# Third attention on single-pass products of split parts, its seams moved off VectorE, with a pair of unread products in every second unit

## The chip, the cores and the metric

One Trainium2 chip, of which the kernel uses one core. A core has five engines that run beside each other: TensorE (PE, matrix products), VectorE (DVE), ScalarE (ACT), GpSimd (POOL) and SyncE (SP, which issues most of the DMAs). Products are written to PSUM, eight banks of 128 x 512 fp32 each. The metric is the time on the device in microseconds (us), one launch; the lower, the better.

## The reference

The whole program is four layers of an attention and a feed-forward part each, on x of shape (4, 512, 128) in fp32. Three layers and the mixture of experts behind the third attention are untouched. What the change touches is the attention of the last layer, with 16 heads of 8 numbers:

```python
xn = (x - mu) / sqrt(var + EPS) * ln_gamma + ln_beta
q, k, v = split(xn @ W_qkv.T + b_qkv)          # (4, 16, 512, 8) each
scores = q @ k.T / sqrt(8)
probs = softmax(scores)
out = (probs @ v) @ W_out.T + b_out
```

The kernel's x before it comes from a mixture of experts (`f30`), whose two results per token are added first, and its result goes through the router of the next mixture (`f31`). The residual is added in the kernel's own form: x, its normalized rows and the output row are added beforehand, the projected attention last.

## The kernel before

**Units.** `attention` (L601) serves three layers. For the last one (tag `a3_`) it works in 16 units: four batches of 512 rows, and four groups of four heads. The heads of a group lie in four row strips of 32 partitions, so that four products with 32 rows of contraction can run in TensorE at the same time.

**Two passes over the scores.** The softmax needs the largest score of each query before the exponentials. `largest` multiplies q by k with queries on the partitions (`s_a`, 16 products of 32 x 512 a unit), and VectorE reduces each (`low<-s_a`, L721). `lowered` transposes the negated maxima on TensorE (`low_a`, L727) and adds them to q in rows that the heads of this unit leave unused (`ql_a`, L730); k has ones in those rows. `by_key` multiplies the other way round, keys on the partitions (`t_a`, 16 products), so that the maximum is subtracted inside the product, and ScalarE takes the exponentials out of PSUM (`w_a`, L741). `times_values` multiplies them by v and a column of ones (`acc_a`, L837). `summed` copies the sums, `normalized` transposes them (`ot_a`, L856) and divides, `gathered` and `ended` transpose and project a whole batch, and `residual` adds it to x.

**Number format.** `factors` gives fp32 operands, for which TensorE records two instructions a product, unless the unit is in `parts`; then the operands are `fp32r`, one instruction a product. The first attention works that way: q and k are split into a rounded part (hi) and the rest (lo), and the four strips of a head's 32 rows hold hi and lo so that one product makes the sum of the parts' products. The rows take this shape on a round trip through DRAM (`to_units`, `unit_qk`). The third attention passes no `parts` before the change.

**Order.** PE, DVE, ACT and POOL run in the order of the program text in this stage; SP's queue is ordered by a scheduler. A half-round is two products of `largest` for a later unit, two of `by_key` for the current one, interleaved, and the values of an earlier round; eight half-rounds make a unit:

```python
together(step(largest, n + lead), step(by_key, n))
```

with `lead` of ten half-rounds. The first unit has an order of its own (`first_unit`). The loop over units also puts in its pieces of other work: `begin(b)`, a generator that combines the mixture's results, normalizes x, and makes q, k and v of the next batch a piece at a time; `go_on`, the router of `f31` for a finished batch; `normalized`, `gathered`, `ended`; and `beside`, which writes zeros over the DRAM rows of `f31` (two times 2080 KB and once 2048 KB, L285) from SP's queue.

**Per unit.** `start` calls `project`, which masks q on ScalarE (`q_a`, L1019) and k on POOL (`k_a`, L1699) for the unit's group.

Of the kernel before, what the change touches and what calls it, by code (L numbers as in the profile page):

```python
# [9 lines left out]
FP = mybir.dt.float32  # L10
# [32 lines left out]
def kernel(ctx: ExitStack, tc: tile.TileContext, a: dict, out: bass.AP):  # L43
# [202 lines left out]
    class Mixture:  # L246
# [289 lines left out]

        def combine(self, b):

            for j in range(self.k):
                row = 1 + j * T + b * S  # L540
                r = work.tile([P, NT, D], FP, name=f"r{j}{b}_{self.tag}", tag="n", bufs=3)
                nc.sync.dma_start(r, self.res[row : row + S, :].rearrange("(t p) d -> p t d", p=P))
                nc.vector.tensor_tensor(xs[b], xs[b], r, ALU.add)
            yield
# [47 lines left out]

    lows = []

    def rows_of_largest(pool):
        for i in range(2):
            low = pool.tile([P, NT, P], FP, name=f"low{i}", tag=f"low{i}", bufs=1)
            nc.gpsimd.memset(low, 0.0)
            lows.append(low)

    def attention(pool, tag, begin, project, residual, owT, added, after=None, beside=(), fetch=None, parts=None):  # L601

# [17 lines left out]

        def product(ps, q, k, r, i, n0, n1, as_=FP):
            nc.tensor.matmul(  # L622
                ps[:, n0:n1],
                q[r : r + SLOT, i * P : (i + 1) * P].bitcast(as_),
                k[r : r + SLOT, n0:n1].bitcast(as_),
                start=True,
                stop=True,
            )

        def factors(u):  # L630

            if parts is not None and units[u] in parts:
                return *parts[units[u]], FR
            return *st["qk", u], FP
# [75 lines left out]
        def largest(u, i, rs):  # L710
            q, k, as_ = factors(u)
            out = []
            if i == 0 and rs[0] == 0:
                st["low", u] = lows[u % len(lows)]
            for r in rs:
                ps = bank(f"s_{tag}{u}_{i}{r}")
                yield lambda ps=ps, r=r: product(ps, q, k, r * SLOT, i, 0, S, as_)
                out.append((ps, r))
            for ps, r in out:
                c = r * SLOT + (units[u][1] + 1) % NG * HD  # L720
                nc.vector.tensor_reduce(st["low", u][:, i, c : c + 1], ps, AX.X, ALU.max, negate=True)  # L721

        def lowered(u, n0=0, n1=S):
            q, k = st["qk", u]
            ps = bank(f"low_{tag}{u}")
            for i in range(n0 // P, n1 // P):
                nc.tensor.transpose(ps[:, i * P : (i + 1) * P], st["low", u][:, i, :], ident)  # L727
            if n0 == 0:
                st["ql", u] = pool.tile([P, S], FP, name=f"ql_{tag}{u}", tag="ql", bufs=2)
            nc.vector.tensor_tensor(st["ql", u][:, n0:n1], ps[:, n0:n1], q[:, n0:n1], ALU.add)  # L730

        def by_key(u, j, rs):
            q, k = st["qk", u]
            out = []
            for r in rs:
                ps = bank(f"t_{tag}{u}_{j}{r}")
                yield lambda ps=ps, r=r: product(ps, k, st["ql", u], r * SLOT, j, 0, S)
                out.append((ps, r))
            for ps, r in out:
                w = pool.tile([P, S], FP, name=f"w_{tag}{u}_{j}{r}", tag="w", bufs=8)  # L740
                nc.scalar.activation(w, ps, AF.Exp)  # L741
                st["w", u, j, r] = w
# [49 lines left out]
        def first_unit():  # L792
# [19 lines left out]
            together(top[10], other[0, 1])  # L812
            start(2)
            together(top[11], other[0, 0])
            for j in range(2, NT):
# [51 lines left out]
        def gathered(b):  # L867
            oT = pool.tile([P, S], FP, name=f"oT_{tag}{b}", tag="ou", bufs=3)
            copy(oT, transposed(st["o", b].rearrange("p t g c -> p t (g c)"), f"oT_{tag}{b}"))
            st["oT", b] = oT  # L870
# [3 lines left out]
        def ended(b):  # L874
            po = bank(f"proj_{tag}{b}").rearrange("p (t d) -> p t d", d=D)
            for t in range(NT):
                nc.tensor.matmul(po[:, t, :], st["oT", b][:, t * P : (t + 1) * P], owT, start=True, stop=True)
            residual(b, po)
# [3 lines left out]
        def go_on():  # L882
            if rest and next(rest[0], "end") == "end":
                rest.pop(0)

        def begin_next(u, between=False):
# [8 lines left out]
        with tc.manual_schedule(engines={E_.PE, E_.DVE, E_.Activation, E_.Pool}):  # L895
# [14 lines left out]
            for u in range(0 if added else 1, n_units + 1):  # L910
                last = u - 1
                now, nxt = u < n_units, u + 1 < n_units
                for j in range(NT):
# [30 lines left out]
                    elif not begin_next(u):  # L944
                        go_on()
                    if j % 2:
                        next(beside, None)
# [11 lines left out]

    def values(b, nT, wvT, bias, tag):  # L960

# [6 lines left out]
        if bias is None:  # L968
            nc.vector.tensor_copy(dst, src.rearrange("p t h d -> p (t h) d"))
        else:  # L970
# [33 lines left out]

    def heads(pool, nT, mixed, bT, tag):

# [3 lines left out]
        q = pool.tile([P, S], FP, name=f"q_{tag}", tag="q")  # L1010
        nc.vector.tensor_scalar(q, ps[0], float(HD) ** -0.5, bT[:, 0:1], ALU.mult, ALU.add)
        k = pool.tile([P, S], FP, name=f"k_{tag}", tag="k")
# [66 lines left out]
    def to_units(parts, tag, queues):  # L1079
# [3 lines left out]
        for (hi, lo), name, order, queue in zip(parts, "qk", halves, queues):  # L1083
            rows = dram.tile([NG, 4, 4, HD, S], FP, name=f"{name}rows_{tag}", tag=f"{name}rows_{tag}")
            for c, x in enumerate(order):
                queue.dma_start(rows.rearrange("g h c d s -> c (g h) d s")[c], (hi, lo)[x])
            out.append(rows)
        return out

# [537 lines left out]
    def prep_l3_attn():  # L1627
        qkv = head_weights(a["L3_attn_W_qkv"], a["L3_attn_b_qkv"], "l3")
        owT = load_T(a["L3_attn_W_out"], D, D, "ow3T", "owT")
        ob = load_row(a["L3_attn_b_out"], "ob3", "ob")  # L1630
        gr = stage.tile([2, D], FP, name="gb_rows", tag="gb_rows", bufs=1)
        nc.sync.dma_start(gr[0:1, :], a["L3_attn_ln_gamma"].unsqueeze(0))
# [7 lines left out]
    def l3_attn(summed, beside, after):  # L1640
        (mixed, bT, wvT, bv), owT, ob, gb = l3["attn"]
        with tc.tile_pool(name="attn3", bufs=2) as pool:
            qk = {}

            def begin(b):
                tag = f"a3_{b}"
                yield from summed(b)

# [5 lines left out]
                for t in range(NT):  # L1654
                    nc.vector.bn_stats(st[:, t, :], xs[b][:, t, :])
                    nc.vector.bn_aggr(mv[:, t, :], st[:, t, :])
                    if t == 1:
                        yield
# [27 lines left out]
                yield  # L1686
                qk[b] = heads(pool, nT, mixed, bT, tag)
                yield
                values(b, nT, wvT, bv, tag)
                nc.gpsimd.tensor_tensor(xs[b], xs[b], n, ALU.add)  # L1690
                add_row(b, ob)

            def residual(b, po):
                nc.vector.tensor_tensor(xs[b], po, xs[b], ALU.add)

            def project(b, g):
                q, k = qk[b]
                kg = pool.tile([P, S], FP, name=f"k{g}_a3_{b}", tag="kg", bufs=4)
                nc.gpsimd.tensor_scalar(kg, k, own[:, g : g + 1], next_row[:, g : g + 1], ALU.mult, ALU.add)  # L1699
                return unit_q(pool, q, g, f"a3_{b}"), kg  # L1700

            attention(pool, "a3_", begin, project, residual, owT, None, after, beside(pool))

# [188 lines left out]
```

## Time and profile before

| | |
|---|---|
| median of 3 runs | 1484.34 us (1476.2 to 1484.8) |
| the profiled execution | 1488.5 us, of it 1486.8 us from the first to the last instruction |
| PE busy, whole span | 1233.2 us (83%) |
| DVE, ACT, POOL busy, whole span | 889.7, 681.7, 695.9 us |
| mean granted clock of TensorE | 0.905 |
| the third attention's scores and values | about 1068 to 1368 us of the span |

A row of the timeline gives the start, the time, the engine, the line of the kernel, what is written and read by the names of the program (numbers left out), the shapes, how many instructions were merged, and, in brackets, how long the engine had been idle and what ended that. A row of the window view gives, for a stretch of time, its length, the busy time of each engine, the clock that TensorE was granted (1.00 is full), and what the DMA engines did. Matmuls are pipelined and overlap, so the time that a product takes from the others is read from start to start, and not from its own length. SPq and ACTq rows are DMAs issued from those engines' queues.

### The profile page before, as it was taken

How to read it: one execution, taken by the hardware profiler on the slowest of the kernel's cores; microseconds unless marked ns; L12 is line 12 of the kernel's file. 1: busy time of each engine (PE TensorE's matmuls, PEld its weight loads, DVE VectorE, ACT ScalarE, POOL GpSimd, SP SyncE). 2: the span in 40 equal slices, each digit the busy share in tenths (PEclk: the TensorE clock that was granted, in tenths of full speed). 3: DMA queues.
4: the chain of work that ended last, by engine and by line, in shares of the span. 5: the costliest groups of instructions: out<-in, count | busy, mean ns of one | idle time of the engine just before them, and what ended most of it. 6: DMA issues, size and time to landing. Idle time of an engine off the chain costs nothing.

```text
span 1486.8 us, 27646 instructions
## 1 busy us (share of the span) xinstructions
PE 1233.2 (83%) x9882; PEld 774.1 (52%) x9882; DVE 889.7 (60%) x3109; ACT 681.7 (46%) x1434; POOL 695.9 (47%) x813
## 2 busy tenths in 40 slices
PE   5786999986979899989899588359599999997494
PEld 4464766765756566666565244237353334332273
DVE  5226877762346667776468867434478787772252
ACT  2334977862442377776522122123246565553041
POOL 5444878962524777876441213645421242213253
PEclk9996999996989999999999777579799999997597
DMA  8423673103424684430220000132105000000333
GB/s 252 125 60 108 194 259 110 52 18 89 136 60 87 189 264 149 129 94 17 58 58 1 0 0 9 35 101 74 41 11 184 9 15 1 16 1 15 79 85 108
DMA packets 109548, 122.40 MB, mean 82 GB/s; under 512 B 10038, under 2 KB 74788, under 8 KB 109412
## 3 DMA queue, kind: packets, MB, share of 16 engines
q1 hardware_dynamic: 97892, 103.22, 24.1%
q0 software_dynamic: 6656, 13.22, 2.7%
q10 hardware_dynamic: 4864, 4.20, 1.1%
q8 instruction: 79, 1.29, 0.4%
q14 instruction: 57, 0.47, 0.1%
HBM read 70.36 MB, written 50.24 MB: 81 GB/s over the span
## 4 chain that ended last, share of the span: by engine, by line
PE 63%; DVE 14%; DMA 7%; POOL 7%; issue 5%; ACT 2%; SPq 2%; POOLq 0%; ACTq 0%; DVEq 0%
PE s_a L622 11%; PE t_a L677 8%; PE h_f L491 6%; PE o_f L527 6%; PE acc_a L837 5%; PE acc_a L699 4%; DVE x L1583 3%; PE t_a L622 3%; PE gu_f L1351 2%; POOL disp_f L417 2%; PE y_f L1552 2%; PE gu_f L1352 2%; PE o_f L1386 2%; PE ot_a L856 2%; DVE sc_a L653 1%
## 5 line engine op out<-in xcount | busy, mean ns | idle before, releaser
L664 POOL TENSOR_SCALAR sc_a<-sc_a,top_a 128x128 f32<-128x128 f32 (+3 forms) x256 | 276.5, 1095 | 72.6 <-DVE top_a L649 42.4
L622 PE MATMUL s_a<-k_a,q_a 32*128 32x512 f32 (+3 forms) x1280 | 240.6, 538 | 16.7 <-DMA k_a<-krows_a 6.8
L721 DVE TENSOR_REDUCE low<-s_a 128x1 f32<-128x512 f32 x256 | 163.0, 684 | 44.5 <-PE t_a L622 30.3
L741 ACT ACTIVATE w_a<-t_a 128x512 f32<-128x512 f32 x240 | 131.9, 596 | 108.8 <-PE t_a L622 71.9
L677 PE MATMUL t_a<-ident,sc_a 128*128 128x128 f32 x1280 | 172.0, 281 | 6.6 <-DVE top_a L653 6.2
L513 POOL DMA_INDIRECT res_f<-y_f,back_f x112 | 107.0, 956 | 136.8 <-ACT y_f L512 95.7
L677 PEld LDWEIGHTS t_a<-ident,sc_a 128*128 128x128 f32 x1280 | 143.6, 144 | 32.1 <-issue 12.2
L622 PE MATMUL t_a<-ql_a,k_a 32*128 32x512 f32 x480 | 158.9, 644 | 0.4 <-DVE low L721 0.3
L666 ACT ACTIVATE sc_a<-sc_a,top_a 128x128 f32<-128x128 f32 (+3 forms) x256 | 134.4, 576 | 17.1 <-DVE top_a L653 12.9
L622 PEld LDWEIGHTS s_a<-k_a,q_a 32*128 32x128 f32 x1280 | 85.3, 185 | 86.7 <-issue 47.5
L686 ACT ACTIVATE w_a<-t_a 128x256 f32<-128x256 f32 (+2 forms) x192 | 94.4, 527 | 61.2 <-PE t_a L677 60.3
L417 POOL DMA_INDIRECT disp_f<-n_f,to_f x96 | 95.4, 994 | 45.3 <-issue 34.9
L527 PE MATMUL o_f<-w_l,h_f 128*128 128x128 f32 (+1 forms) x896 | 110.4, 278 | 2.4 <-ACT h_f L495 2.3
L491 PE MATMUL h_f<-dT_f,w_l 128*128 128x320 f32 (+1 forms) x256 | 106.9, 556 | 2.8 <-ACT dT_f L469 2.8
L527 PEld LDWEIGHTS o_f<-w_l,h_f 128*128 128x128 f32 (+1 forms) x896 | 102.5, 184 | 11.4 <-ACT h_f L495 4.3
L699 PE MATMUL acc_a<-w_a,vpad 128*32 128x128 f32 x2560 | 97.6, 278 | 0.7 <-ACT w_a L686 0.6
L688 ACT COPY w_a<-t_a 128x256 f32<-128x256 f32 (+2 forms) x192 | 93.4, 526 | 6.0 <-PE t_a L677 5.9
L173 POOL TENSOR_SCALAR rs_f<-mv_f 128x4 f32<-128x4 f32 (+1 forms) x23 | 5.4, 233 | 184.7 <-DVE mv_f L170 184.5
L653 DVE CUSTOM_DVE_ANT_0 sc_a<-s_a,future 128x128 f32<-128x128 f32 (+3 forms) x128 | 62.4, 487 | 45.0 <-PE s_a L622 39.4
L512 ACT ACTIVATE y_f<-o_f,d_f 128x128 f32<-128x128 f32 (+1 forms) x112 | 39.0, 394 | 105.8 <-DVE o_f L507 99.1
L837 PE MATMUL acc_a<-w_a,vpad 128*32 128x256 f32 x1024 | 83.7, 398 | 2.4 <-ACT w_a L741 2.1
L1398 POOL TENSOR_TENSOR h_f<-h_f,cb_f 128x512 f32<-128x512 f32 x32 | 40.6, 1285 | 80.7 <-DVE h_f L1357 41.2
(366 smaller groups left out, 2215.7 us busy)
## 6 DMA issues: line engine op xcount, KB each, us to landing
fac_a<-fac_a_sb SPq DMA_DIRECT2D x36, 256.0 KB
disp_f<-zeros_f SPq DMA_DIRECT2D x4, 2080.0 KB
d_f<-disp_f SPq DMA_DIRECT2D x32, 260.0 KB
w_l<-in_L_ffn_w_dram SPq DMA_DIRECT2D x16, 512.0 KB
cb_f<-rows_f SPq DMA_DIRECT2D x16, 512.0 KB
q_a<-fac_a SPq DMA_DIRECT2D x32, 256.0 KB
k_a<-fac_a SPq DMA_DIRECT2D x32, 256.0 KB
r_f<-res_f SPq DMA_DIRECT2D x16, 256.0 KB
```

Of the source, the lines that this page charges most:

```text
L417: nc.gpsimd.indirect_dma_start(out=self.to[c][i0 + t][:, :], out_offset=bass.IndirectOffsetOnAxis(ap=to[:, c, t : t + 1], axis=0), in_=ns[ ...
L491: nc.tensor.matmul(ps[u][:, :cap], w1[:, e, (c + u) * P : (c + u + 1) * P], dT, start=True, stop=True)
L513: nc.gpsimd.indirect_dma_start(out=self.back[e * per + s][:, :], out_offset=bass.IndirectOffsetOnAxis(ap=back[:m, s : s + 1], axis=0), in_ ...
L527: nc.tensor.matmul(po[:m, s, :], h[:, c, s * P : s * P + m], w2[:, e, c, :], start=(c == 0), stop=(c == NC - 1),)
L622: nc.tensor.matmul(ps[:, n0:n1], q[r : r + SLOT, i * P : (i + 1) * P].bitcast(as_), k[r : r + SLOT, n0:n1].bitcast(as_), start=True, stop= ...
L664: nc.gpsimd.tensor_scalar(sc, sc, top, None, ALU.subtract)
L666: nc.scalar.activation(sc, sc, AF.Exp, bias=top, scale=-1.0)
L677: nc.tensor.transpose(ps[:, x * n + j * P : x * n + (j + 1) * P], st["sc", u, i, r0 + x][:, j * P : (j + 1) * P], ident,)
L699: nc.tensor.matmul(st["acc", u][r * SLOT : (r + 1) * SLOT, i * P : (i + 1) * P], vpads[b % 2][:, j, g * 4 + r, :], st["w", u, i, r][:, j * ...
L721: nc.vector.tensor_reduce(st["low", u][:, i, c : c + 1], ps, AX.X, ALU.max, negate=True)
L741: nc.scalar.activation(w, ps, AF.Exp)
L837: nc.tensor.matmul(acc[r * SLOT : (r + 1) * SLOT, n0:n1], vpads[b % 2][:, j, g * 4 + r, :], st["w", u, j, r, half] if ("w", u, j, r, half) ...
```

## The change

It does five things in the third attention.

1. Units 1 to 15 take their operands as parts. `to_heads` splits q and k of a batch into hi (ScalarE) and lo (POOL), and writes each four-fold to DRAM, eight DMAs of 256 KB; `unit_parts` reads two tiles of 256 KB for each unit, three units ahead, from SP's queue. Products of `largest` and `by_key` are then `fp32r`. Unit 0 stays as it was. `project` does nothing for units in parts.
2. The maximum cannot ride in q's rows any more. `lowered` splits the 16 maxima of a row into two parts on VectorE, transposes them, and ScalarE copies them out as `less`; `by_key` adds them with a second product on the same PSUM bank, whose other operand is a constant of ones and zeros (`two`, made once on POOL).
3. Work at the seams between batches moves. Adding the mixture's results to x goes from VectorE to POOL for batches 1 to 3; q, the values and the transposed sums go from VectorE to ScalarE; the residual becomes a product of x with the identity into the projection's bank, and a copy on ScalarE. The statistics of a batch are taken one tile at a time.
4. The bias of the values is no longer added to each batch's values; its product with the output weights is added to the output row once, before the stage.
5. `busy` multiplies the identity by itself, 128 x 512, twice, in fp32, in the second round of each odd unit, into a bank that nobody reads.

```diff
-        def combine(self, b):
+        def combine(self, b, engine=nc.vector):
...
-                nc.vector.tensor_tensor(xs[b], xs[b], r, ALU.add)
+                engine.tensor_tensor(xs[b], xs[b], r, ALU.add)
...
+        two = pool.tile([P, 2, P], FP, name="two", tag="two", bufs=1)
+        nc.gpsimd.memset(two[:, 0], 0.0)
+        for r in range(4):
+            nc.gpsimd.memset(two[r * SLOT : r * SLOT + 2, 0, :], 1.0)
+        nc.gpsimd.tensor_copy(two[:, 1].bitcast(FR), two[:, 0])
+        twos.append(two[:, 1])
...
         def lowered(u, n0=0, n1=S):
...
+            if in_parts(u):
+                top = st["top", u]
+                hi, lo = (low.rearrange("p t (r c) -> p t r c", c=SLOT)[:, :, :, x] for x in range(2))
+                nc.vector.tensor_copy(hi.bitcast(FR), top)
+                nc.vector.tensor_tensor(lo, top, hi, ALU.subtract)
             ps = bank(f"low_{tag}{u}")
...
+            if in_parts(u):
+                st["less", u] = pool.tile([P, S], FP, name=f"less_{tag}{u}", tag="less", bufs=2)
+                nc.scalar.copy(st["less", u].bitcast(FR), ps)
+                return
...
         def by_key(u, j, rs):
-            q, k = st["qk", u]
+            q, k, as_ = factors(u)
...
-                yield lambda ps=ps, r=r: product(ps, k, st["ql", u], r * SLOT, j, 0, S)
+                yield lambda ps=ps, r=r: product(ps, k, q, r * SLOT, j, 0, S, as_, True)
                 out.append((ps, r))
             for ps, r in out:
+                rows = slice(r * SLOT, (r + 1) * SLOT)
+                yield lambda ps=ps, rows=rows: nc.tensor.matmul(
+                    ps, twos[0][rows, :].bitcast(FR), st["less", u][rows, :].bitcast(FR), start=False, stop=True
+                )
...
+        def busy(u):
+            ps = bank(f"busy_{tag}{u}")
+            for x in range(2):
+                nc.tensor.matmul(
+                    ps.rearrange("p (t d) -> p t d", d=P), ident, bc_mid(ident, [P, NT, P]), start=True, stop=True
+                )
...
+                    if on_pe and j == 1 and u % 2:
+                        busy(u)
...
+    def to_heads(pool, qk, tag, queues):
+        out = []
+        for x, name, order, queue in zip(qk, "qk", halves, queues):
+            hi, lo = (pool.tile([P, S], FP, name=f"{name}{y}_{tag}", tag=f"{name}{y}", bufs=1) for y in ("hi", "lo"))
+            nc.scalar.copy(hi.bitcast(FR), x)
+            nc.gpsimd.tensor_tensor(lo, x, hi, ALU.subtract)
+            rows = dram.tile([4, NG, 4, HD, S], FP, name=f"{name}rows_{tag}", tag=f"{name}rows_{tag}")
+            for c, y in enumerate(order):
+                queue.dma_start(rows.rearrange("h g c d s -> c (h g) d s")[c], (hi, lo)[y])
+            out.append(rows.rearrange("h g c d s -> g h (c d) s"))
+        return out
+
+    def unit_parts(pool, rows, g, tag, bufs):
+        out = []
+        for r, name in zip(rows, "qk"):
+            t = pool.tile([P, S], FP, name=f"{name}{g}_{tag}", tag=f"{name}parts", bufs=bufs)
+            nc.sync.dma_start(t, r[g])
+            out.append(t)
+        return out
...
+        nc.tensor.matmul(ps[:, :D], bv.to_broadcast([P, P]), owT, start=True, stop=True)
+        nc.vector.tensor_tensor(ob, ps[:, :D], ob, ALU.add)
...
-                yield from summed(b)
+                yield from summed(b, nc.gpsimd if b else nc.vector)
...
-                    if t == 1:
+                    if t == 1 or b > 0 and t < NT - 1:
                         yield
...
-                qk[b] = heads(pool, nT, mixed, bT, tag)
+                qk[b] = heads(pool, nT, mixed, bT, tag, b > 0)
+                if b > 0:
+                    rows[b] = to_heads(pool, qk[b], tag, (nc.sync, nc.sync))
                 yield
-                values(b, nT, wvT, bv, tag)
+                values(b, nT, wvT, None, tag, b > 0)
+                if b == 0:
+                    rows[b] = to_heads(pool, qk[b], tag, (nc.sync, nc.scalar))
                 nc.gpsimd.tensor_tensor(xs[b], xs[b], n, ALU.add)
                 add_row(b, ob)
...
             def residual(b, po):
-                nc.vector.tensor_tensor(xs[b], po, xs[b], ALU.add)
+                flat = xs[b].rearrange("p t d -> p (t d)")
+                nc.tensor.matmul(po.rearrange("p t d -> p (t d)"), ident, flat, start=False, stop=True)
+                nc.scalar.copy(xs[b], po)
...
             def project(b, g):
+                if (b, g) in parts:
+                    return None
...
+            def fetch(b, g):
+                if (b, g) != (0, 0):
+                    parts[b, g] = unit_parts(pool, rows[b], g, f"s_a3_{b}", 4)
```

In the order that the program text and SP's scheduler make of it: on POOL the two `lo` of batch 0 stand ahead of the two additions to its x, and those ahead of unit 0's k; on SP the read of unit 4's q is followed by the first of the three zero transfers, and the read of its k stands behind that; each pair of `busy` stands between the second and the third round (four half-rounds in, of eight) of units 1, 3, 5 and so on to 15 in PE's order.

## The prediction

> **What bounds the kernel now.** I read the window view first: it puts the third attention, its 13 middle units, on TensorE.
>
> ```profile
> core 0: us, PE busy (x) PEld busy (x) DVE busy (x) ACT busy (x) POOL busy (x), PEclk, DMA share, GB/s
> 1111.60:1338.40 226.80, 225.49 (x1897) 87.67 (x1895) 175.92 (x372) 133.52 (x245) 57.17 (x91) 1.00 0.11 37
> ...
> 1111.58 0.60 PE L856 MATMUL ot_a<-ident,ou_a 128*128 128x128 f32 x4
> ...
> 1338.36 0.66 PE L856 MATMUL ot_a<-ident,ou_a 128*128 128x128 f32 x4
> ```
>
> The two `ot_a` rows are the same step 13 units apart: 226.8 / 13 = 17.4 us a unit. PE has no free time and its clock is granted in full. VectorE works 175.9 / 13 = 13.5 us a unit, ScalarE 10.3. The timeline then shows one half-round (a unit has eight) and, below it, a group of four products in the first attention, which already multiplies parts in one pass.
>
> ```profile
> 1298.24 0.69 PE L622 MATMUL s_a<-k_a,q_a 32*128 32x512 f32 x1
> ...
> 1298.78 0.59 PE L622 MATMUL s_a<-k_a,q_a 32*128 32x512 f32 x1
> ...
> 1299.32 0.64 PE L837 MATMUL acc_a<-w_a,vpad 128*32 128x256 f32 x8
> ...
> 1299.44 1.08 ACT L741 ACTIVATE w_a<-t_a 128x512 f32<-128x512 f32 x2 [0.37 <-PE t_a L622]
> 1299.89 0.69 PE L622 MATMUL s_a<-k_a,q_a 32*128 32x512 f32 x1
> ...
> 270.10 0.51 PE L622 MATMUL s_a<-k_a,q_a 32*128 32x512 f32 x4
> 270.54 0.66 PE L677 MATMUL t_a<-ident,sc_a 128*128 128x128 f32 x4
> ```
>
> From start to start: four fp32 products at once, in two instructions each, take 1299.32 - 1298.24 = 1.08 us, the values (`acc_a`) 0.57; together 1.65. Four single-pass products take 270.54 - 270.10 = 0.44. Both fit 0.21 fixed plus 0.213 a pass (estimates from 0.44 and 1.08: three passes more cost 0.64).
>
> **The change, part by part.**
>
> *Score products, units 1 to 15.* The maxima need one pass[...]. The weights need one pass, then one more on the same rows for `less`. The two kinds run side by side, so a half-round is 0.21 + 2 x 0.213 + 0.57 = 1.21 us: 0.43 less, 3.4 a unit.
>
> *What is late next.* The reductions. The Trainium skill, "TensorEngine Tiling (Array Packing)", section PSUM Bottleneck, speaks against the change: faster products do not empty PSUM faster. The row: two reductions in 1.26 to 1.29 us when alone, four in a row in 2.52. So VectorE needs about 1.25 a half-round, just above PE's 1.21. By PE alone a half-round gives 0.43, by the rule 0.39, and nothing is left to absorb anything else. I take the rule's side: VectorE's remaining rows now stand beside PE's remaining rows with little slack.
>
> *A unit's sums.* PE: 8 x 1.21 = 9.7; `low` and `ot`, 0.59 each, 1.2; per batch transposes, projections, routing 7.5 plus the new residual product 0.96 (half of `qk_a`'s pair below), over four units 2.1; half a busy pair 0.96. Together 13.9. VectorE: 13.5, less `ql` 0.69, less a quarter of combine 1.4, q 0.75, values 0.69, residual 0.69, oT 0.68 (1.0), plus two 16-wide operations (0.2 each by the small rows): 12.3. ScalarE: less `qg` 0.74, plus `less` 0.59 and a quarter of q, two hi copies, values, oT, residual (3.7): about 11. Before, PE's own sum was 8 x 1.65 + 1.2 + 1.9 = 16.3 of 17.4 measured: 1.1 of friction, while VectorE had 0.4 free in every half-round. Now it has none. Ends: 13.9 (all extras hidden) and 16.6 (VectorE's 10.0 of reductions, its other 2.3 and PE's 4.3 beside the half-rounds, one after another). Before, the same two ends are 16.3 and 19.8 (13.2 + 3.1 of PE, 3.5 of VectorE), and it ran at a third of the way; a third is 14.8 here. Seams (below) add 0.2: 15.0. **13 units x 2.4 = 32 us gained.**
>
> *The busy pair* (odd units, fp32, 128x512, four instructions).
>
> ```profile
> 1230.12 1.98 PE L1009 MATMUL qk_a<-nT_a,wmixed_l 128*128 128x512 f32 x4
> ```
>
> The next start is at 1232.04: 1.92 us, eight times, 15 us of PE, in the sum above. Can it pay? The Trainium skill, "TensorE: Matmul & The Clock Gate", section on why this matters, says gaps under about 3 us cost no clock. Here is a gap of 1.85 us (895.4 to 897.25) with the clock at half right after, while short transposes and eight-column products ran:
>
> ```profile
> 894.00:898.00 4.00, 2.15 (x10) 1.00 0.01 2
> 898.00:902.00 4.00, 3.84 (x18) 0.66 0.00 0
> 902.00:906.00 4.00, 4.00 (x10) 0.50 0.00 0
> ```
>
> By the rule the pair is pure cost; by the row a gap of 2 us can cost some 4 us of half clock. But in the first attention, PE mostly 85 to 100% busy, single-pass products included, the clock stayed at 1.00 but for one dip. I price clock losses at 2 us (0 to 25).
>
> *Start of the stage.* Unit 0's k tile is queued on POOL behind work that did not stand there.
>
> ```profile
> 1067.09 0.69 ACT L1013 ACTIVATE k_a<-qk_a,bmixed_l 128x512 f32<-128x512 f32 x1 [3.57 <-PE qk_a L1009]
> ...
> 1067.88 3.03 POOL L1699 TENSOR_SCALAR k_a<-k_a,own,next_row 128x512 f32<-128x512 f32 x4 [1.90 <-ACT k_a L1013]
> 1068.70 4.82 PE L622 MATMUL s_a<-k_a,q_a 32*128 32x512 f32 x24 [0.76 <-POOL k_a L1699]
> ```
>
> After: qhi on ScalarE to 1068.4, then on POOL `qlo`, `klo` (1.27 each, the row of a 128x512 tensor operation), the two additions to x that were over by 1066 (1.26 each), then k at 1073.5. First scores 5.6 us later. **Lost 5.6.** The first and second units then win back: 18 products of units 1 and 2 beside fp32 halves (4), six cheaper half-rounds (2), combine off VectorE (1), less one busy pair (1.9): **gained 5.**
>
> *Rows through DRAM.* Eight 256 KB writes a batch (four for batch 0's k from ScalarE's queue, whose exponentials wait 4 us later anyway) and two 256 KB reads a unit, three units ahead. The first attention does the same: last `klo` write issued from 126.45, products on the fetched rows at 137.34, 11 us. For unit 1 that ends near 1082, its scores are due near 1085: hidden. For unit 4 it is not: on SP's queue its q read is followed by the 2080 KB of zeros, and its k read only then; SP also waits there for POOL's zero tile, behind two additions. Before, the three zero transfers filled 20 us at 309 GB/s, so one takes 7. From batch 1's qk: writes about 9, zeros 7, read 2, 18 us; the scores are six half-rounds, v and `ot` later, 12. **A wait of 6 us** (0 to 9). Batches 2 and 3 have two units of time. Unit 5's rows pass the second zeros with about 4 us to spare.
>
> *Seams.* ScalarE gets q, k, two hi copies and values, 3.2 us in a row, with exponentials behind them; PE waits there for PSUM, about 1 us a batch: the 0.2 a unit above. POOL's combine (2 x 1.28) ends before the statistics that VectorE waits with.
>
> *Tail.* The last units save 0.43 in eight half-rounds; the last residual product at low clock and its copy cost 1.5. **Gained 2.** The bias product, `two` (in POOL's 13.4 us idle before 994.78) and fewer `kg`, `qg` cost nothing: PE waits for DMA or POOL there.
>
> **Sum.** -32 + 5.6 - 5 + 6 - 2 + 2 = -25 us. The profiled execution took 1488.5 (span 1486.8): 1463. It lies 4 us above the median of the three runs, 1484.34, off which the same saving gives 1459; I say **1460**.
>
> **Rivals.**
> 1. *Clean overlap.* PE and VectorE hide each other's extras, the unit falls to 14.1, the unit 4 wait to 3. For it: ScalarE has 4 us a unit to spare and VectorE 2.7, so a late start can be caught up. Against: before never reached its own sum. Another 12 + 3 us, 1445.
> 2. *PSUM hand-off.* A half-round takes four of eight banks, the values one, each seam one more, so PE can run only one half-round ahead and extras add up: a unit of 16.3. For it: in before the fourth product of many half-rounds already starts 0.25 late. 13 x 1.3 = 17 lost of the gain, unit 4's wait at 9: 1480.
> 3. *Clock, the slow side.* Waits at unit 4 and at the seams drop the clock, and half-clock PE becomes the bound again. PE's 13.9 become some 24 at half clock (`qk_a` took 3.39 cold, at 1063.66, against 1.98): 9 a unit over the forecast's 15. Over 14 units each 0.1 of mean clock lost (a fifth of the time at half) costs 25: from 0.90 down the gain is gone, at 0.83 the time is 1502. Against: 1.00 over 227 us now, about 0.99 in the first attention.
> 4. *The busy pair does nothing for the clock,* which would be 1.00 without it. The forecast stands either way.
>
> **How the numbers follow.** Forecast 0.52, clean overlap 0.16, hand-off 0.20, clock 0.12. This measurement tells about 1% (15 us) from no change; below 1469.5 is faster. Forecast and overlap are, nearly all; hand-off is mostly the same. Faster 0.67, same 0.21, slower 0.12. The forecast's own range, friction 14.2 to 15.9, is 1448 to 1472; to hold 8 in 10 it goes from overlap to past hand-off: 1440 to 1488.
>
> **What would show it.** Units of 15 us between `ot_a` rows; half-rounds near 1.25 with reductions back to back; first scores 5 to 6 us after k; one wait of PE for a DMA at unit 4's first scores; clock at or near 1.00. Wrong if units stay above 16.5, if the clock drops below 0.95 in mid-stage, or if another fetch is late.

## The result, and the profile after

The changed kernel takes 1516.95 us (1515.31 to 1520.22) where the kernel before takes 1481.94: ratio 1.0244, 95% interval 1.0205 to 1.0283. I had said 1460, a ratio of 0.984. Measured again later beside the experiments it stood at 1.0142 (1.0097 to 1.0186). So it is slower, by 1.4 to 2.4%, and two ratios of this kernel can lie 1% apart. The experiments were run in four sets, on four chips, each set with the kernel before beside it; the changed kernel itself stands only in the last set, so the others are compared with it by their ratio to the kernel before, and I call nothing a difference that is well under 1%. The ratios leave out executions more than 1.5% slower than the fastest of their version (one of the run without pairs, one of the run with the early split, three of the run with three moves); medians and ranges keep them.

The profiled execution took 1516.24 us (span 1514.5), 27.7 us of span more than before. The window view shows where: first the start of the stage (first transposes to the first `ot_a` row), then the 13 units that were 226.8 us before, and last 20 us out of these that ran undisturbed.

```profile
core 0: us, PE busy (x) PEld busy (x) DVE busy (x) ACT busy (x) POOL busy (x), PEclk, DMA share, GB/s
1065.08:1124.80 59.72, 49.43 (x277) 25.17 (x277) 32.81 (x63) 20.28 (x38) 10.13 (x12) 0.66 0.22 71
1124.80:1370.13 245.33, 214.79 (x1724) 92.49 (x1720) 160.01 (x373) 141.85 (x263) 65.28 (x97) 0.85 0.26 86
1265.00:1285.00 20.00, 18.80 (x169) 9.02 (x166) 12.96 (x30) 15.63 (x30) 10.55 (x14) 1.00 0.37 118
```

The units take 245.3 / 13 = 18.9 us, not 15.0. TensorE (PE) now has 30 us in them without work, and its clock, 1.00 before, is 0.85; in the start it is 0.66 (0.88 before). In the third row, without waits, the clock is full. There the timeline shows the half-rounds that I had forecast:

```profile
1267.06 0.50 PE L628 MATMUL s_a<-k_s_a,q_s_a 32*128 32x512 f32 x1
...
1267.39 0.40 PE L764 MATMUL t_a<-less_a,two 32*128 32x512 f32 x2
1267.72 0.64 PE L867 MATMUL acc_a<-w_a,vpad 128*32 128x256 f32 x8
1268.29 0.50 PE L628 MATMUL s_a<-k_s_a,q_s_a 32*128 32x512 f32 x1
```

From 1267.06 to 1268.29 is 1.23 us. The four products take 0.33 of it, the second products with `less` another 0.33, where four fp32 products took 1.08. The saving is there. What eats it is in the waits of TensorE over the stage (what it waited for; us in total, times, longest):

```profile
PE low_a L745 <- DVE low L742: 16.3, 15, 2.4
PE T_a L196 <- ACT n_a L1744: 13.8, 1, 13.8
PE s_a L628 <- DMA k_s_a<-krows_a: 13.5, 1, 13.5
PE s_a L628 <- POOL k_a L1781: 6.3, 1, 6.3
```

The second row stood in the profile before as well (13.86). The fourth I had forecast (5.6), the third in part (6). The first I had not. It comes once a unit, and one instance shows what it does:

```profile
1236.15 1.28 DVE L734 TENSOR_REDUCE top_a<-s_a 128x1 f32<-128x512 f32 x2
1237.34 0.17 DVE L741 CAST low<-top_a 128x16 fp32r<-128x16 f32 x1
1237.55 0.19 DVE L742 TENSOR_TENSOR low<-top_a,low 128x16 f32<-128x16 f32 x1
...
1237.80 0.66 PE L745 MATMUL low_a<-ident,low 128*128 128x128 f32 x4 [1.30 <-DVE low L742]
```

The split of the maxima (`CAST` and `TENSOR_TENSOR` on VectorE) stands in program order behind two reductions of the half-round just issued, which belong to a later unit. TensorE, with nothing else in its queue, waits 1.30 us. Then the windows around it:

```profile
1232.00:1236.00 4.00, 3.76 (x37) 1.68 (x40) 3.79 (x13) 2.36 (x5) 0.00 (x0) 1.00 0.00 0
1236.00:1240.00 4.00, 2.70 (x22) 1.71 (x16) 2.45 (x11) 1.47 (x3) 0.38 (x2) 0.79 0.01 4
1240.00:1244.00 4.00, 4.00 (x28) 1.41 (x28) 3.41 (x10) 2.17 (x4) 0.91 (x1) 0.50 0.18 52
...
1248.00:1252.00 4.00, 4.00 (x17) 1.51 (x18) 1.67 (x4) 1.09 (x3) 3.04 (x4) 0.50 0.10 33
1252.00:1256.00 4.00, 4.00 (x37) 1.51 (x35) 1.97 (x3) 1.08 (x2) 2.88 (x3) 1.00 0.15 52
```

The clock falls to half and stays there for some 14 us, although TensorE is busy for 4.00 of every 4 us. It comes back with the pair of unread products, which starts at 1249.94. A busy column of 4.00 is no sign of a full clock; only the PEclk column shows it.

### The profile page after: what moved, and what is told of

The parts are those of the page before. It is cut to its first block, busy times and chain, and to the rows that moved or that the text cites. A ratio compares the mean times of both kernels' runs of the same rounds, so it can differ in the third digit from the quotient of the medians.

```text
span 1514.5 us, 27413 instructions
## 1 busy us (share of the span) xinstructions
PE 1228.5 (81%) x9684; PEld 783.5 (52%) x9684; DVE 871.5 (58%) x3107; ACT 691.7 (46%) x1454; POOL 702.9 (46%) x818
## 4 chain that ended last, share of the span: by engine, by line
PE 55%; DVE 18%; POOL 9%; DMA 8%; issue 6%; ACT 2%; SPq 1%; POOLq 0%; another core or an unknown queue 0%; DVEq 0%; ACTq 0%
PE t_a L686 8%; PE s_a L628 7%; PE h_f L491 5%; PE o_f L527 5%; PE acc_a L708 4%; PE acc_a L867 4%; DVE x L1652 3%; DVE top_a L734 3%; PE y_f L1621 2%; POOL disp_f L417 2%; PE t_a L764 2%; POOL res_f L513 2%; PE gu_f L1420 1%; PE busy_a L924 1%; DMA cb_f<-rows_f 1%
## 5 line engine op out<-in xcount | busy, mean ns | idle before, releaser
L734 DVE TENSOR_REDUCE top_a<-s_a 128x1 f32<-128x512 f32 x240 | 152.4, 684 | 86.9 <-PE s_a L628 44.3
L628 PE MATMUL s_a<-k_a,q_a 32*128 32x512 f32 (+3 forms) x800 | 101.2, 480 | 20.3 <-DVE top_a L662 6.5
L867 PE MATMUL acc_a<-w_a,vpad 128*32 128x256 f32 x1024 | 94.0, 442 | 2.3 <-ACT w_a L769 2.3
L628 PE MATMUL s_a<-k_s_a,q_s_a 32*128 32x512 f32 x240 | 71.1, 568 | 13.8 <-DMA k_s_a<-krows_a 13.5
L628 PE MATMUL t_a<-q_s_a,k_s_a 32*128 32x512 f32 x240 | 75.5, 549 | 2.4 <-DVE top_a L734 1.8
```

Of the source, the lines that this page charges most:

```text
L628: nc.tensor.matmul(ps[:, n0:n1], q[r : r + SLOT, i * P : (i + 1) * P].bitcast(as_), k[r : r + SLOT, n0:n1].bitcast(as_), start=True, stop= ...
L734: nc.vector.tensor_reduce(st["top", u][:, i, r : r + 1], ps, AX.X, ALU.max, negate=True)
L867: nc.tensor.matmul(acc[r * SLOT : (r + 1) * SLOT, n0:n1], vpads[b % 2][:, j, g * 4 + r, :], st["w", u, j, r, half] if ("w", u, j, r, half) ...
```

## The experiments

**Theory A:** waits of TensorE are the loss, at the start, at unit 4's rows and at the late split, together with the half clock that each starts; the pair is only work. **Rival B:** single-pass work brings the half clock by itself, whatever the waits. **Rival C:** the pairs keep the clock up. **Rival D:** VectorE is the pacemaker, so that a wait taken away comes back at the next reductions. In the first four runs each takes one suspect away.

**No pairs.**

```diff
-                    if on_pe and j == 1 and u % 2:
-                        busy(u)
```

> The changed kernel without the eight pairs of unread products. Theory A (the loss is waits of TensorE at the start of the stage, at unit 4's rows and at the transposes of the maxima, and the half clock that follows each of them; the pair is only work): the pairs took 2.0 to 3.8 us each, 20 us in all, a part of it beside VectorE's reductions, so 1516.9 falls by 8 to 18 us, to 1499 to 1509, clock about as it was (0.87). Rival C (the pairs keep the clock up): the mean clock falls below 0.86, the spells at half clock get longer, and the time is 1517 or more.

1500.24 us (1487.5 to 1512.41), ratio 1.0127 (1.0085 to 1.017): not to be told from the changed kernel's 1.0142, but 17 us better than its first 1.0244, so what the pairs cost in time stays open between the two. What they do to the clock is plain. After a wait of 1.30 us, the same place as above looks like this:

```profile
1210.00:1218.00 8.00, 6.47 (x58) 2.53 (x56) 7.62 (x25) 4.58 (x9) 0.00 (x0) 0.98 0.00 2
1218.00:1255.00 37.00, 36.76 (x229) 13.98 (x229) 23.50 (x56) 18.55 (x34) 16.34 (x22) 0.50 0.13 44
```

37 us at half clock, 99% busy; it ends where the next batch's transposes stand. The stage's mean clock is 0.74, with pairs 0.82 and 0.88 (two profiles). So rival C is right about the clock, and theory A, for which the pair is only work, is wrong about it.

**Zeros earlier.** The zeros of `f31` are written before batch 1's rows.

```diff
-    def emptied(*mixes):
+    def emptied(*mixes, behind=4):
...
-                for _ in range(4):
+                for _ in range(behind):
                     yield
                 mix.zeroed(pool, "ou", 3)
...
-        l3_attn(f30.combine, emptied(f31), lambda b: f31.tokens([b], l3["gate"], "gpsimd", fine=True))
+        l3_attn(f30.combine, emptied(f31, behind=2), lambda b: f31.tokens([b], l3["gate"], "gpsimd", fine=True))
```

> The changed kernel with the zeros of f31 written two pieces earlier, so that on SP's queue they stand behind unit 3's rows and ahead of batch 1's. Theory A: TensorE's wait for unit 4's k rows falls from 13.5 us to about 4 (the last write was issued at 1145.8, the read needs about 6 us from there, and the scores were due at 1147.9), the half clock from 1161 to 1181 becomes shorter too: 10 to 18 us less, 1499 to 1507. Rival B (single-pass work by itself brings the half clock, whatever the waits): 9 us less at most, and the clock stays at half for the 15 us behind unit 4's first scores. If the zeros then collide with unit 1's to 3's rows, a new wait of TensorE for a DMA shows before unit 4 and the gain is below 5.

1489.86 us, ratio 1.0106 (1.0064 to 1.0148). The wait went from 13.5 to 11.7 only, where I had expected 4: the zeros were not its main cause. In the DMA rows and TensorE's timeline:

```profile
1127.03 1.60 SPq L1146 DMA_DIRECT2D krows_a<-klo_a  x2
...
1131.99 2.86 SPq L1155 DMA_DIRECT2D k_s_a<-krows_a  x2
...
1142.12 0.76 PE L628 MATMUL s_a<-k_s_a,q_s_a 32*128 32x512 f32 x1 [11.74 <-DMA k_s_a<-krows_a]
```

The last write is issued by 1128.6, the read can go at 1132 when the writes have landed, and the product starts ten us after that. In these ten us the DMA engines moved 131 GB/s (214 during the writes) for several reads of 256 KB queued together. I had priced a read at 2 us; why they take so long was not found.

**Unit 0's k first.** `project(0, 0)` is called ahead of `to_heads`, and its result kept for `start(0)`.

```diff
                 if b == 0:
+                    early[b] = project(b, 0)
                     rows[b] = to_heads(pool, qk[b], tag, (nc.sync, nc.scalar))
```

> The changed kernel with unit 0's masked q and k issued ahead of the splits into parts and of the two additions to x. Theory A: the first scores come 5 to 6 us earlier, and the half clock from 1088 to 1104, which follows TensorE's idle time from 1074 to 1081, is gone too: 6 to 14 us less, 1503 to 1511. Rival B: 5 to 6 us less at most; the half clock stays. A third case: batch 0's rows then come 3 us later and unit 1's scores wait for them, and nothing is gained.

1495.04 us, ratio 1.0172 (1.0129 to 1.0216): it lies between the changed kernel's two ratios, so no gain can be told. The third case happened. The wait for POOL is gone, and unit 1's first scores now wait for their rows:

```profile
PE s_a L628 <- DMA k_s_a<-krows_a: 19.2, 2, 13.9
```

19.2 less 13.9 is 5.3 us for unit 1. Its rows had been hidden only behind the late k.

**Split early.** The two VectorE instructions go ahead of the next reductions; the transposes stay.

```diff
+                        if j == NT - 1 and nxt:
+                            split(u + 1)
                         together(step(largest, n + lead), step(by_key, n))
```

> The changed kernel with the split of the maxima on VectorE (cast and subtraction) issued ahead of the next two reductions, not behind them; the transposes stay where they are. Theory A: TensorE's wait for the split, 16.3 us in 15 times, falls to 5 or less, and the half-clock spells in the middle of the stage that start behind it (1240 to 1252, 1308 to 1324) go: 11 to 25 us less, 1492 to 1506. Rival B: 11 us less at most, and spells of 12 to 16 us at half clock stay in the middle of the stage. Rival D (VectorE is the pacemaker, so a wait taken away here comes back at the next reductions): less than 4 us.

1471.8 us, ratio 0.9991 (0.9964 to 1.0017). This one move gives back the whole loss against the kernel before. TensorE's waits at the split, and then a window of 168 us in mid-stage:

```profile
PE low_a L748 <- DVE low L742: 4.0, 3, 1.5
```

```profile
1150.00:1318.00 168.00, 164.63 (x1496) 73.16 (x1494) 139.39 (x322) 120.98 (x224) 51.69 (x80) 1.00 0.23 77
```

12 us of waits are gone, and by the ratios (0.9991 against 1.0142) it gains 22. The rest fits the clock, but only on average. The mean clock of the whole kernel, over all executions, is 0.888 against 0.883; time at half clock, twice what the mean lacks of 1.00 times the length, is then some 20 us less. The profiled stage does not show it: the 168 us in its middle are at 1.00, but spells at both ends make 82 us at half clock in the stage, where the two profiles of the changed kernel have 115 and 76. Rival D falls; of theory A, the wait is shown here, its half clock is not shown by this run alone.

**All three moves, with and without pairs.**

> The changed kernel with the three moves of the last runs together: zeros earlier, unit 0's k first on POOL, the split of the maxima ahead of the next reductions. Theory A (waits, and the half clock that each starts): the gains add, about 30 to 50 us below the changed kernel, 0.975 to 0.99 of the kernel before; the middle of the stage at clock 1.00 as in the run with the early split. Theory E (single-pass products in strips of 32 rows leave TensorE so near the edge that it drops to half clock at any small break, eight-column products included, and comes back only at a block of full 128-row fp32 products): spells at half clock remain where short products stand (router, ranks), each ends at a pair or at qk, and the time stays above 0.99 of before.

> The same three moves, without the pairs of unread products. If the pair is only work (my prediction's rival 4, and theory A where no half clock is left to end): 8 to 15 us faster than with it. Theory E: every half-clock spell now lasts until the next qk, 30 us and more as in the run without the pairs, and it is 5 to 25 us slower than with them, at a mean clock lower by 0.02 or more.

With pairs 1472.68 us, 0.9975 (0.9942 to 1.0009); without 1464.24 us, 0.9932 (0.9901 to 0.9962). The gains do not add: 0.9975 cannot be told from the early split alone (0.9991). With pairs the clock is 1.00 from batch 2's qk to the end of the stage; without them one spell of some 10 us came after the router's short products and ended by itself. The whole stage has 44 us at half clock with pairs, 73 without. So with the waits at the split gone (those for rows, 12 and 5 us, are still there) the pairs still work on the clock, and cost about what they bring or 6 us more; the intervals overlap. That the run without them would be 5 to 25 us slower, theory E's forecast, did not come true.

**Batch 1 begun earlier.** `begin(1)` runs eight of its ten pieces in the first unit; the early split and unit 0's k stay; zeros between unit 3's rows and batch 1's.

```diff
             together(top[10], other[0, 1])
+            begun(1)
```

> Early split and unit 0's k first, and batch 1 is begun in the first unit (eight of its ten pieces there), with all zeros written between unit 3's rows and batch 1's. The first run with the zeros moved showed that zeros were not what made unit 4's rows late (11.7 in place of 13.5 us): from the last write to the landed k row took 14 us, ten of them in reads at about 100 GB/s. If lateness of batch 1's qk is the cause, the wait for unit 4's rows goes to under 3 us, and the 15 to 30 us of half clock around it go as well: 10 to 25 us below the run of the three moves. If the round trip takes longer when begun earlier (behind the zeros), the wait stays above 8.

1454.1 us, 0.989 (0.9849 to 0.9931). Unit 4 still waits 7.5 us: batch 1's writes stood behind the zeros. The same without pairs, and then with the zeros after unit 5's rows as well:

```diff
-        l3_attn(f30.combine, emptied(f31, behind=0, at_once=True), lambda b: f31.tokens([b], l3["gate"], "gpsimd", fine=True))
+        l3_attn(f30.combine, emptied(f31, behind=5), lambda b: f31.tokens([b], l3["gate"], "gpsimd", fine=True))
```

> The run with batch 1 begun in the first unit, less the pairs of unread products. If they are only work where no half clock is left to end: 4 to 12 us less than with them (0.981 to 0.986 of before). If they keep the clock up, it falls below 1.00 in the middle of the stage, and the time is the same or more.

> The run with batch 1 begun in the first unit, without the pairs, and with the zeros of f31 after unit 5's rows (there the zeros stood ahead of batch 1's writes, which then took 15 us to issue in place of 6). Theory A: unit 4's wait for its rows falls from 7.5 us to under 2, clock at 1.00 from unit 2 on, 0.975 to 0.985 of the kernel before. If reads at about 100 GB/s are slow by themselves, 4 us and more of the wait stay, 0.985 to 0.99. If the clock needs the pairs, spells of 30 us at half clock are back and it is above 0.99.

1452.18 us, 0.983 (0.9762 to 0.9899), and 1445.09 us, 0.9829 (0.9764 to 0.9894). Without the pairs the clock falls again (79 us at half in the stage, 38 with them, two spells of 27 us among them), and again the time is not longer. In the second run the wait for unit 4's rows is gone altogether, yet the ratio is the same; in its profile three spells of half clock (7, 7 and 10 us) came around units 4 to 6. Since its stage is shorter than the other's and has less half clock (52 us), they do not explain why the ratio stayed; with intervals of 0.7% either way that is open.

**Rows alone.** To price the late rows in the changed kernel itself, nothing but batch 1's earlier start and the later zeros was put into it.

> The changed kernel with nothing but batch 1 begun in the first unit and the zeros after unit 5's rows; pair, late split, POOL's order and the seams stay as they are. If the wait for unit 4's rows and its half clock are a term of their own: TensorE's wait of 13.5 us is gone and 10 to 25 us with it, 1.007 to 1.018 of the kernel before, and the spells behind the late split stay. If the late split's half clock swallows the gain (the next 1.3 us wait starts half clock anyway), less than 8 us.

1474.54 us, 1.0011 (0.9986 to 1.0037): 1.3% or 19 us below the changed kernel, here in the same set. The 13.5 us wait has left the list, the split's waits have not (13.4). The whole stage in the profiles, first the changed kernel of this set, then this run:

```profile
1061.73:1369.77 308.04, 266.53 (x2155) 120.31 (x2155) 197.43 (x455) 174.63 (x323) 83.51 (x119) 0.88 0.25 84
1057.98:1353.97 295.99, 271.14 (x2154) 122.20 (x2155) 197.27 (x455) 174.75 (x323) 83.52 (x119) 0.87 0.26 87
```

It is 12 us shorter, about the wait itself, and its clock is no higher: the spell around unit 4 is gone, others came. Over all executions the mean clock of the kernel is 0.887 against 0.883. Either of the two suspects, taken away alone, brings the time back to that of before.

**Is it the wait or the kind of product?** The kernel before, fp32, gets one copy on VectorE ahead of its transposes, so that it waits as the changed kernel does.

```diff
+            if n0 == 0 and n1 == S:
+                low = st["low", u].rearrange("p t c -> p (t c)")
+                nc.vector.tensor_copy(low, low)
             ps = bank(f"low_{tag}{u}")
```

> The kernel before, fp32 products, with one copy of the 128x512 tile of maxima onto itself on VectorE ahead of their transposes, so that TensorE waits about 1.3 us once a unit, as it does in the changed kernel. Theory A (such a wait starts half clock, whatever the products): spells of 10 us and more at half clock appear in the middle of the stage, mean clock there 0.85 to 0.95, and the time rises by 30 us or more, 1.02 and above. Theory E (single-pass products stand nearer to the edge; fp32 ones do not): the clock stays at 1.00 in the middle, and the time rises by the waits alone, 10 to 20 us, 1.007 to 1.014.

1493.09 us, 1.0138 (1.0096 to 1.0179). TensorE's waits from unit 1 on, and then the clock in three windows that cover 12 units:

```profile
PE low_a L730 <- DVE low L727: 15.7, 13, 1.6
```

```profile
1111.18:1185.98 74.80, 69.56 (x586) 26.70 (x584) 55.51 (x108) 41.40 (x76) 16.27 (x26) 1.00 0.28 97
1185.98:1261.46 75.48, 70.40 (x592) 27.37 (x588) 58.52 (x131) 41.60 (x77) 23.47 (x37) 1.00 0.03 8
1261.46:1332.52 71.06, 66.55 (x578) 25.78 (x575) 53.45 (x115) 40.06 (x75) 15.15 (x25) 1.00 0.03 9
```

Thirteen waits of up to 1.6 us, and the clock never leaves 1.00; the time rises by 20 us, about the waits themselves. Waits of the same size start half clock in the changed kernel. So theory A is incomplete, and rival B, as I first had it, is wrong too (168 us of single-pass work ran at 1.00). What fits is both together, theory E as a description: beside single-pass products in strips of 32 rows, a wait of 1.3 us can be enough. The length alone does not decide: in the changed kernel a wait of 1.43 us (to 1205.05) was followed by no half clock, while the two in mid-stage that were, 1.30 and 1.29, have the router's short rank products (0.7 to 0.8 us) right behind them. In the fp32 run these stand behind waits of 1.13. Which property of the products matters was not tested.

**Seams.** First alone in the kernel before, then taken back out of the changed kernel, then out of the run with the zeros after unit 5's rows. Two of the five edits that put them back:

```diff
-                yield from summed(b, nc.gpsimd if b else nc.vector)
+                yield from summed(b)
...
-                qk[b] = heads(pool, nT, mixed, bT, tag, b > 0)
+                qk[b] = heads(pool, nT, mixed, bT, tag)
```

> The kernel before with the seams of the change alone: additions of the mixture's results on POOL, q, values and transposed sums on ScalarE, residual as a product, bias of the values folded; no parts, no pair, fp32 products as before. VectorE had about 4 us a unit free before, so work taken off it brings nothing, and TensorE gets about 1 us a batch more: 0.998 to 1.006 of before. If VectorE's seams had been holding TensorE up (friction of 1.1 us a unit in my sum), up to 12 us less, 0.992.

> The changed kernel with the seams alone put back on VectorE (as in the run that was 1% faster than its neighbour). If ScalarE's seams are a loss of their own (3.2 us in a row ahead of exponentials, at each batch): 4 to 15 us faster than the changed kernel. If the seams only mattered there by chance of a half-clock spell: the same within 5 us.

> The same as the last, but with the seams back on VectorE (additions of the mixture's results, q, values, transposed sums, residual: 4.2 us a batch). My prediction made VectorE the pacemaker once the products are single-pass; then 2 to 4 us a batch come back, and the waits of TensorE for the maxima with them: 0.5 to 1% slower than the run before. If ScalarE's seams cost as much as VectorE's (its exponentials wait behind them), the two are the same within 0.3%.

1471.41 us, 1.0001 (0.9978 to 1.0024), then 1496.09 us, 1.0117 (1.0064 to 1.017): no effect in either. In the third, VectorE's own seams give 1432.98 us, 0.9728 (0.9682 to 0.9773), against 0.9829: about 1% faster, where I had expected slower, though the intervals overlap a little. Its profile has two spells of 3.4 us at half clock in the middle of the stage, that of its neighbour the three longer ones. Why the seams on ScalarE should bring them was not settled.

**The changed kernel and the fastest version once more.**

> The changed kernel itself once more, as the one to compare with on this chip: 1.02 to 1.028 of the kernel before.

> The fastest of the runs once more, five rounds: parts from the second unit, early split, unit 0's k first, batch 1 begun in the first unit, zeros after unit 5's rows, seams on VectorE, no pairs. 0.968 to 0.978 of the kernel before, if the first measurement holds.

1495.27 us, 1.0142 (1.0097 to 1.0186), less than expected, and 1436.19 us, 0.9731 (0.9696 to 0.9766). The fastest version beats both kernels, the kernel before by 37 us. In the stage of its profile 31 us are at half clock (before: 19), without a pair: the moves together do take the half clock away that none of them took away alone. Its units from the first `ot_a` row on:

```profile
1118.21:1321.69 203.48, 196.12 (x1832) 87.80 (x1828) 171.21 (x401) 146.49 (x273) 57.41 (x88) 0.98 0.29 99
```

15 units in 203.5 us, the short last one included, with 4.1 us of waits at the split and 6.2 at unit 1's rows left in the stage.

## Why the prediction was wrong, point by point

- **Half-rounds and the unit's sum: right in size.** Forecast 1.21 to 1.25 us a half-round and 15.0 a unit; measured 1.23, and 14.6 a unit over ten units at full clock in the run with three moves. That is 2.8 us a unit saved, if the unit runs undisturbed. The terms within were partly luck: I had 0.21 fixed plus 0.213 a pass, resting on three passes more for an fp32 product, which no row shows; the rows show 0.33 twice, and the sums, 0.64 and 0.66, agree.
- **"What is late next": the right engine, the wrong place.** I put VectorE's reductions beside TensorE as a rate, 1.25 us against 1.21. I added the two 16-wide operations of the split to VectorE's sum (0.4 us) and never asked what stands ahead of them. They were queued behind two reductions (1.28), and TensorE has nothing to do until they end. That is 16.3 us of waits with no term in my sum: the diff shows a new wait, and its queue was not walked through.
- **Clock, 2 us (0 to 25): the failing step.** It took some 27 (the sum is below). Stage mean 0.97 before; 0.82 after and 0.88 in the second profile. From 328.9 us (first transposes to last `ot_a`) to 308.0 in that second profile of the same program, the time at half clock, twice what the mean lacks, falls by 40 us (from 115 to 76): 0.53 us lost for each us at half. My rival 3 priced it at 25 us for each 0.1 of the stage's mean clock, from 1460 up: that gives 1505 at 0.82 and 1490 at 0.88, where the two profiled executions took 1516 and 1492. So its price was near, and its kind of cause, waits that drop the clock, fits; but it named unit 4 and the seams, not the split. I gave it 0.12 because the first attention's single-pass work had run at 1.00. That was a poor comparison: no wait for a split once a unit stands there, and of waits for the maxima (`top_a`) its profile lists seven in all, 1.4 us at most.
- **The rule and the row.** I weighed the Trainium skill, "TensorE: Matmul & The Clock Gate", "Why this matters for your kernels" (no gaps above some 3 us), against a row with 1.85 us and half clock behind it, and then took neither as a price. The run of fp32 products with waits up to 1.6 us agrees with the rule; in the changed kernel 1.3 us was enough, against it. The page's section "A second HAM failure mode: psum-queue depth-cycling", which I had not used, comes nearer: in a bf16 kernel that cycles through PSUM banks, short pauses between groups of products are frequent enough for the clock to swing between half and full. It does not explain this case alone, since the same cycling ran at 1.00 for 168 us with the early split.
- **The pair: priced as 15 us of pure work, worth about its cost.** Without it the time is the same or up to 17 us shorter, and mid-stage spells last 20 to 38 us instead of some 14. Rival 4 was wrong for the changed kernel.
- **Start, +5.6: right (6.3) and empty.** Taking it away exposed unit 1's rows, 5.3 us late, which I had called hidden. The first two units, forecast even after the start, lost 9 us to the first `ot_a` (59.7 against 50.5), at a clock of 0.66.
- **Unit 4's rows, 6 (0 to 9): 13.5, and zeros were not the main reason.** The mis-sized terms: qk ran at half clock (3.78 us), so the first write was issued 5.0 us after its start; the reads took about 10 us, not 2. 1.3% of the time hung on it, of which the stage's profiles show the wait itself.
- **Seams, 1 us a batch: not seen.** Moving them off VectorE brought no gain in three comparisons.
- **The rest.** Of the 27.7 us of span, 25.7 lie in the stage. It began 4 us later than before, but in runs with the same code ahead of it it began anywhere from 1049.8 to 1064.9, so I give no cause.

In numbers: waits above the forecast are 16.3 + 7.5 = 24 us, those at the split without any term in the sum. The forecast stage, some 278 us (303.2 less 25), was exceeded by 51. The other 27, where I had 2, are put down to half clock by difference; 96 us more than before were spent at half clock, part of it inside the waits.

## What to carry to other kernels

When a change makes an engine's work lighter, walk the queue of every instruction that the engine then waits for: two tiny operations in program order behind another unit's reductions cost some 22 us here, what eight units saved. Read the granted clock beside the busy time, since lighter products can be 99% busy at half clock; the waits in front of them cost about twice their length by the ratios (12 us of waits, 22 us of time), though no single profile shows the second half. Of a round trip through DRAM, measure write, landing and read separately before moving anything out of its way.

## What the runs showed of the hardware

- In the changed kernel's profile, four of the five waits of 1.29 us or more at the split were followed by half clock within 3 us, for 10 to 14 us; the fifth, 1.43 us, was not. Thirteen waits of 1.2 us on average, 1.6 at most, before fp32 products in the same strips of 32 rows were followed by none. What TensorE's clock counts was not measured.
- Once at half clock, single-pass work 99% busy stayed there for 37 us. In the changed kernel's two profiles the mid-stage spells of 10 us and more ended at a pair or a qk product or within 3 us behind it; shorter ones, and in versions without pairs some of up to 27 us, ended alone.
- In all profiles the spells lasted near 3.4 us times a whole number (7, 10, 14, 17, 24, 27 us). The Trainium skill, "TensorE: Matmul & The Clock Gate", "What's actually happening", gives a free-running window of about 3.4 us; these lengths agree with it.
- Reads of 256 KB, several queued together, took ten us to land at 131 GB/s in the run with the zeros earlier, where the same kernel had just written at 214. With zeros among them the engines moved 339 GB/s in the same place of the changed kernel (1151 to 1161 us), and the reads were no quicker.
